# Attention block and large-kernel convolution on one core: padding columns left out, a mixed operand, and a new order of the first loads

## The chip, the cores and the metric

The kernel runs on one core of a Trainium2 chip. The metric is the device time of one execution in microseconds (us); the time before is the median of three runs. Beside it stands one profiled execution, from which all durations are read.

## What is computed

The input x has 384 channels of 192 x 192 pixels in float32. Two layers follow each other, each added to its own input:

```
x = x + L0(gn(x))        # gn: group normalization, 32 groups of 12 channels
x = x + L1(gn(x))

L0: qkv = w_qkv (1152 x 384) times the channels of every pixel, + bias
    2x2 max-pool  -> 96 x 96;  depthwise 3x3;  split in q, k, v
    8 heads of 48 channels: attn = normalized q times normalized k (48 x 48),
    four top-k softmaxes (24, 32, 36, 38 kept), summed with gains, times v
    exact GELU, 2x upsampling, w_proj (384 x 384), + bias
L1: sum of seven depthwise convolutions (13x13, and six dilated ones that fit
    inside 13x13), each with its own batch normalization
```

A head's 48 channels lie across the boundaries of the 128-channel tiles: heads 2 and 5 have channels in two tiles each.

## The kernel before, in words

**Stage 1, statistics (first 166 us).** The mean and variance of every channel are needed before anything can be normalized. The first 16 image rows are loaded as four large tiles xt (`load`, L160, on SP's DMA queue), which stay for the next stage. The rest comes as 66 blocks xs of 128 x 1536 (`load_block`, L201), on SP's queue for even numbers and ACT's for odd ones, ten buffers ahead. VectorE runs bn_stats over the four xt tiles (L230 to L234) and then over the 66 blocks in order (L235 to L241), with one bn_aggr for each channel tile (L243), and `group_stats` (L106) turns this into a scale and shift. Meanwhile GpSimd folds the seven convolution kernels into one (L217 to L225) and stores it as wfd (L226). The weights wqk and wv are loaded on SP's queue (L273, L274); these two lines lie outside a block of `manual_schedule`, so the framework's scheduler places them, and it placed them among the xs loads.

Inside a block of `tc.manual_schedule()` each engine executes its instructions in the order of the program text.

**Stage 2, attention (166 to 1951 us).** A list of steps (L629) goes twice over 24 blocks of the image: 12 steps a block for q and k, then six for v. A step is one `project` (L333, 12 records on TensorE) and its `pool` (L349). Depthwise taps (`taps`, L379, VectorE), `begin`, `end`, transposes (`turn`) and `add_gram` are put into later steps by `at(step, ...)`. In between, `normalize` prepares the next block on ACT, `add_up` forms 2x2 sums on GpSimd, and `strip` (L437) and `clear` (L288) lay out the convolution's tap matrices zd in DRAM: a load of wfd into the still free memory of v for every eighth block, one ACT copy, four DMA issues on GpSimd. The softmaxes (`attend`, L465) run inside the second pass and leave bd, the attention matrix of all heads as one block-diagonal matrix in three channel tiles.

**Stage 3, attention times v (1951 to 2060 us).** For 24 blocks of four rows (L702) TensorE multiplies bd with v. AV_BLOCKS (L47) lists which channel tiles of v each output tile needs: (0, 1), (0, 1, 2) and (1, 2), seven products of 384 columns. ACT applies GELU in place into v, VectorE takes statistics of the stored sums.

**Stage 4, projection (2060 to 2223 us).** 72 blocks (L1013): three products, ACT's copy with bias to pjs and its store to pd, VectorE's cell (L1037) and bn_stats (L1038). The generators in `running` are moved on by one `yield` at every block (`advance`, L991): `derive` (L790), which forms the second normalization's parameters for one channel tile and contains `group_stats` with `rsqrt`; `load_rows` for the convolution's first tiles; `residual` (L906), which adds the upsampled L0 output to the input rows, in parts of three rows on GpSimd here. Then come `patch`, `normalize1` and `arrange` for tile 0.

**Stage 5, convolution (2223 us to the end).** 48 tiles of eight channels (L1089). An image is cut into patches so that the 13x13 kernel is a product with a 128 x 128 matrix for each of five row offsets g: `convolve` (L945) runs five accumulating products of 24 x 12 = 288 columns. The input d is xp, [channel, 51 row groups, 12]; row group 0 and row group 50 lie outside the image and are zeros, set once by `patches` (L761, L762). Offset g reads row groups g, g+2, ..., so group 0 is the first of g = 0 and group 50 the last of g = 4. Around it the loop loads rows and taps ahead (SP), adds residuals (GpSimd), normalizes (ACT), transposes in and out (VectorE) and stores (GpSimd's queue).

Of the kernel before, what the change touches and what calls it, by code (L numbers as in the profile page):

```python
# [14 lines left out]
P = 128  # L15
# [31 lines left out]
AV_BLOCKS = [  # L47
    [
        j
        for j in range(NJ)  # L50
        if any(
            CH * h < P * (j + 1) and CH * (h + 1) > P * j and CH * h < P * (i + 1) and CH * (h + 1) > P * i
            for h in range(HEADS)
        )
    ]
    for i in range(NJ)
]
# [3 lines left out]
def tile_attn_then_large_kernel_conv(ctx: ExitStack, tc: tile.TileContext, a: dict, out: bass.AP):  # L61
# [24 lines left out]
    def rsqrt(pool, v, eps, name, least=None):  # L86

        shape = list(v.shape)
        ve = pool.tile(shape, F32, name=f"{name}_ve")
        if least is None:  # L90
            nc.vector.tensor_scalar(ve, v, eps, None, ALU.add)
        else:
            nc.vector.tensor_scalar(ve, v, least, None, ALU.max)
        sd = pool.tile(shape, F32, name=f"{name}_sd")
        nc.scalar.activation(sd, ve, AF.Sqrt)
        r = pool.tile(shape, F32, name=f"{name}_r")
        nc.vector.reciprocal(r, sd)

        t = pool.tile(shape, F32, name=f"{name}_t")
        nc.vector.tensor_mul(t, r, r)  # L100
        nc.vector.tensor_mul(t, t, ve)
        nc.vector.tensor_scalar(t, t, -0.5, 1.5, ALU.mult, ALU.add)
        nc.vector.tensor_mul(r, r, t)
        return r

    def group_stats(pool, psum, mv, name, js=range(NJ)):  # L106
# [25 lines left out]
        r = rsqrt(pool, var, 1e-5, name)  # L132
# [38 lines left out]
    with (  # L171
# [29 lines left out]
        def load_block(n):  # L201
            j, b = divmod(n, NX)
            xt = sx.tile([P, FB], F32, name=f"xs_{n}", tag="xs")
            eng = nc.sync if n % 2 == 0 else nc.scalar
            eng.dma_start(out=xt, in_=x[j * P : (j + 1) * P, FX + b * FB : FX + (b + 1) * FB])
            xss.append(xt)

        scale = rsqrt(s1, bn[:, :, 3, :], 1e-5, "bn")
# [8 lines left out]
        for j in range(NJ):  # L217
# [8 lines left out]
        nc.gpsimd.dma_start(  # L226
            out=wfd.rearrange("(j p) s -> p j s", p=P), in_=wf.rearrange("p j x y -> p j (x y)")
        )

        for n in range(4):  # L230
            xt = xts[n // 2, n % 2]
            for j in range(NJ):
                nc.vector.bn_stats(stats[:, j, 2 * n, :], xt[:, j, :512])
                nc.vector.bn_stats(stats[:, j, 2 * n + 1, :], xt[:, j, 512:])  # L234
        for n in range(NJ * NX):  # L235
            j, b = divmod(n, NX)
            xt = xss.pop(0)
            for q in range(FB // 512):
                nc.vector.bn_stats(stats[:, j, NS0 + b * (FB // 512) + q, :], xt[:, q * 512 : (q + 1) * 512])  # L239
            if n + 10 < NJ * NX:  # L240
                load_block(n + 10)  # L241
            if b == NX - 1:
                nc.vector.bn_aggr(mv0[:, j, :], stats[:, j].rearrange("p n s -> p (n s)"))  # L243
        nc.vector.tensor_copy(gn0, in_one(group_stats(s1, s_ps, mv0, "g0")))  # L244
# [7 lines left out]
    with ExitStack() as ctx_v:  # L252
# [20 lines left out]
        nc.sync.dma_start(out=wqk, in_=wqkv[:, :, : 2 * C])  # L273
        nc.sync.dma_start(out=wv, in_=wqkv[:, :, 2 * C :])  # L274
# [359 lines left out]
        with tc.manual_schedule():  # L634
            for sb in range(2):
                for j in range(NJ):
                    normalize(0, sb, j)
                    add_up(0, sb, j)
            for s, (B, u, m, sb) in enumerate(steps):
# [11 lines left out]
                if B < NB and u == 3:  # L651
                    strip(b)
                if B + 1 < 2 * NB:
# [31 lines left out]
        with (  # L685
# [13 lines left out]

            with tc.manual_schedule():  # L700
                sms = [load_sums(b) for b in range(2)]
                for b in range(NBB):  # L702
                    if b + 2 < NBB:
                        sms.append(load_sums(b + 2))
                    pss = []
                    for i in range(NJ):
                        ps = b1_ps.tile([P, NBK], F32, tag=f"av{i}", name="av")
                        js = AV_BLOCKS[i]
                        for j in js:
                            nc.tensor.matmul(  # L710
                                ps,
                                lhsT=bd[:, j, i * P : (i + 1) * P],
                                rhs=v[:, j, b * RB : (b + 1) * RB, :].rearrange("p r w -> p (r w)"),
# [3 lines left out]
                        pss.append(ps)  # L717
                    for i in range(NJ):
# [36 lines left out]
        def patches(pool, i):  # L755
# [5 lines left out]
            nc.gpsimd.memset(t[:, :, 0], 0.0)  # L761
            nc.gpsimd.memset(t[:, :, NQ - 1], 0.0)  # L762
# [27 lines left out]
        def derive(i, stats):  # L790
# [27 lines left out]
            for q, t in enumerate((mean, sd)):  # L818
                nc.gpsimd.tensor_copy(sv[:, q], t.unsqueeze(2).to_broadcast([P, nj, P]))
# [86 lines left out]
        def residual(k, n=ME + 1):  # L906

            for m0 in range(0, ME + 1, n):
# [3 lines left out]
                nc.gpsimd.tensor_add(rv, rv, uv.unsqueeze(2).to_broadcast([P, (m1 - m0) * WS, 2]))  # L912
# [32 lines left out]
        def convolve(k, c, co):  # L945
# [3 lines left out]
            for g in range(NGR):  # L949
                o = (NGR - 1 - g) * UQ * BC  # L950
                nc.tensor.matmul(  # L951
                    ps,
                    lhsT=wt[:, c, o : o + P],
                    rhs=d[:, c, g : g + 2 * NT - 1 : 2, :],
                    start=(g == 0),
# [42 lines left out]
        with (  # L998
# [4 lines left out]
            with tc.manual_schedule():  # L1003
# [9 lines left out]
                for n in range(NJ * NBB):  # L1013
# [38 lines left out]
                    if n == NBB + 13:  # L1052
                        running.append(residual(0, 3))
# [11 lines left out]
                    if n == 2 * NBB + 12:  # L1065
                        running.append(residual(1, 3))
                    if n == 3 * NBB - 4:
                        assert next(first, first) is first
# [93 lines left out]
```

## Time and profile before

| what | value |
|---|---|
| median of three runs (range) | 3169.14 us (3168.58 to 3170.71) |
| the profiled execution | 3174.78 us |
| its span, first to last instruction | 3172.9 us |
| mean granted TensorE clock | 0.997 |
| statistics end, first product | 159.1, 166.8 us |
| attention times v | 1951.0 to 2060.2 us |
| projection | 2060.2 to 2223.5 us |
| convolution's products begin | 2223.5 us |

The profile names instructions by line, engine and operation, with output and inputs by the program's names. PE is TensorE, PEld its weight load, DVE VectorE, POOL GpSimd, SP the engine that only issues DMAs. "The chain" is the sequence of work that ended last, followed back from the last instruction. An arrow at the end of a line (`<-`) names what ended the idle time before it. A float32 product appears as two TensorE records. The granted clock (PEclk) is 1.00 at full speed.

### The profile page before, as it was taken

What the parts mean: (1) busy time and instruction counts of PE and PEld (TensorE: products, weight loads), DVE (VectorE), ACT (ScalarE), POOL (GpSimd) and SP (SyncE); (2) the same over time, 40 slices, a digit from 0 to 9 for tenths busy, and PEclk for the clock granted to TensorE, in tenths of its full rate; (3) what the DMA queues carried; (4) which work ended last, traced back from release to release, by engine and by line L of the source; (5) the groups of instructions that cost most, each with busy time, mean ns of one, the idle gap of its engine ahead of it and who ended that gap; (6) DMA issues with size and microseconds to landing.
All of it is one profiled execution on the core that took longest, in us unless ns stands there. A gap on an engine that the chain in (4) does not pass through costs nothing.

```text
span 3172.9 us, 31552 instructions
## 1 busy us (share of the span) xinstructions
PE 2982.8 (94%) x10954; PEld 1971.5 (62%) x10954; DVE 2497.1 (79%) x3387; ACT 1227.9 (39%) x2288; POOL 878.5 (28%) x1044
## 2 busy tenths in 40 slices
PE   0099999999999999999999999999999999999998
PEld 0056666666666666665555555555777777777776
DVE  7968787878878787889998988366788777777775
ACT  0044444444444444444445443323333333333332
POOL 3033232332323223212222221011333343333331
PEclk9999999999999999999999999999999999999999
DMA  9924444343443434333333333376999999999994
GB/s 386 372 84 125 127 122 115 109 121 113 125 128 116 118 111 117 116 103 123 100 97 123 104 109 110 116 213 190 256 256 242 237 244 242 241 244 242 241 215 113
DMA packets 274960, 528.65 MB, mean 167 GB/s; under 512 B 22290, under 2 KB 189664, under 8 KB 274800
## 3 DMA queue, kind: packets, MB, share of 16 engines
q1 hardware_dynamic: 203664, 333.91, 39.1%
q0 software_dynamic: 45104, 152.26, 17.3%
q10 hardware_dynamic: 26032, 40.46, 3.5%
q8 instruction: 86, 1.41, 0.2%
q14 instruction: 74, 0.61, 0.1%
HBM read 365.18 MB, written 161.37 MB: 166 GB/s over the span
## 4 chain that ended last, share of the span: by engine, by line
PE 87%; DVE 8%; DMA 3%; issue 1%; POOL 0%; ACT 0%; SPq 0%; POOLq 0%; DVEq 0%; ACTq 0%
PE qkv L340 48%; PE conv L951 28%; PE pj L1022 4%; PE av L710 3%; DVE v L387 3%; DVE stats L239 2%; PE gram L428 2%; PE tr L416 2%; DVE mx L351 1%; DMA xs<-in_x 1%; DMA xt<-in_x 1%; DMA wqk<-in_wqkvT 1%; DMA pd<-pjs 0%; DMA up<-pd 0%; DMA wt<-zd 0%
## 5 line engine op out<-in xcount | busy, mean ns | idle before, releaser
L340 PE MATMUL qkv<-xt,wqk 128*128 128x384 f32 x3456 | 1133.1, 487 | 1.3 <-ACT xt L317 1.3
L951 PE MATMUL conv<-xp,wt 128*128 128x288 f32 x3840 | 933.1, 406 | 1.2 <-ACT co L959 1.2
L340 PEld LDWEIGHTS qkv<-xt,wqk 128*128 128x128 f32 x3456 | 650.5, 190 | 436.0 <-ACT xt L317 2.1
L951 PEld LDWEIGHTS conv<-xp,wt 128*128 128x128 f32 x3840 | 729.0, 190 | 202.8 <-ACT co L959 1.7
L387 DVE SCALAR_TENSOR_TENSOR acc<-pooled,wd,acc 128x384 f32<-128x384 f32 (+2 forms) x1152 | 720.8, 626 | 30.6
L351 DVE TENSOR_REDUCE mx<-qkv 128x192 f32<-128x768 f32 x432 | 412.7, 955 | 253.4 <-PE qkv L340 241.2
L935 DVE STREAM_TRANSPOSE xp<-xn 128x4608 f32<-128x4608 f32 (+1 forms) x107 | 441.7, 4128 | 190.7 <-PE conv L951 171.6
L358 ACT ACTIVATE pooled<-mx,bq 128x192 f32<-128x192 f32 x432 | 196.8, 456 | 963.9 <-DVE mx L351 963.9
L340 PE MATMUL qkv<-xt,wv 128*128 128x384 f32 x1728 | 563.4, 487 | 1.5 <-ACT xt L317 1.1
L340 PEld LDWEIGHTS qkv<-xt,wv 128*128 128x128 f32 x1728 | 325.7, 190 | 234.3 <-ACT xt L317 7.1
L959 ACT ACTIVATE co<-conv,cb 128x288 f32<-128x288 f32 x384 | 191.3, 499 | 605.5 <-PE conv L951 605.5
L387 DVE SCALAR_TENSOR_TENSOR v<-pooled,wd,v 128x384 f32<-128x384 f32 (+2 forms) x576 | 375.5, 652 | 15.2
L325 POOL TENSOR_TENSOR sum<-xt 128x192 f32<-128x192 f32 x144 | 94.7, 657 | 699.6 <-ACT xt L317 699.1
L317 ACT ACTIVATE xt<-xt,gn 128x768 f32<-128x768 f32 x288 | 284.8, 1013 | 2.9 <-DVE gn L244 2.9
L976 POOL DMA_DIRECT2D out<-o x191 | 105.8, 584 | 585.0 <-DVE o L967 532.2
L912 POOL TENSOR_TENSOR raw<-raw,up 128x2496 f32<-128x2496 f32 (+2 forms) x56 | 241.9, 4325 | 22.4 <-DMA up<-pd 22.4
L967 DVE STREAM_TRANSPOSE o<-co 128x2304 f32<-128x2304 f32 (+1 forms) x50 | 209.8, 4199 | 20.5 <-ACT co L959 20.5
L456 POOL DMA_DIRECT2D zd<-v x96 | 72.0, 757 | 510.9 <-ACT v L447 510.9
L112 PE MATMUL g_ps<-mv,gm 128*32 128x1 f32 x18 | 1.8, 186 | 159.3 <-DVE mv L243 158.6
L1022 PE MATMUL pj<-v,wp 128*128 128x384 f32 x432 | 148.8, 504 | 2.6 <-DVE cell L1037 2.1
L239 DVE BATCH_NORM_STATS2 stats<-xs 128x6 f32<-128x512 f32 x198 | 118.4, 678 | 6.2 <-DMA xs<-in_x 5.4
L1022 PEld LDWEIGHTS pj<-v,wp 128*128 128x128 f32 x432 | 83.8, 197 | 60.4 <-issue 5.1
(165 smaller groups left out, 1751.8 us busy)
## 6 DMA issues: line engine op xcount, KB each, us to landing
xt<-in_x SPq DMA_DIRECT2D x96, 1152.0 KB, 5.6
wt<-zd SPq DMA_DIRECT2D x47, 1536.0 KB, 13.1
raw<-in_x SPq DMA_DIRECT2D x182, 312.0 KB, 12.8
out<-o POOLq DMA_DIRECT2D x188, 288.0 KB, 6.3
zd<-v POOLq DMA_DIRECT2D x96, 416.0 KB, 5.0
up<-pd SPq DMA_DIRECT2D x184, 156.0 KB, 11.8
xs<-in_x SPq DMA_DIRECT2D x33, 768.0 KB, 14.7
xs<-in_x ACTq DMA_DIRECT2D x33, 768.0 KB, 12.3
```

The costliest lines, as they stand in the source:

```text
L239: nc.vector.bn_stats(stats[:, j, NS0 + b * (FB // 512) + q, :], xt[:, q * 512 : (q + 1) * 512])
L317: nc.scalar.activation(xt[:, j], xt[:, j], AF.Identity, bias=gn0[:, j, 1:2], scale=gn0[:, j, 0:1])
L340: nc.tensor.matmul(ps[:, r, : 2 * W], lhsT=wq[:, j, mm * P : (mm + 1) * P], rhs=xt[:, j, r * 2 * W : (r + 1) * 2 * W], start=(j == 0), sto ...
L351: nc.vector.tensor_reduce(mx, ps[:, :, : 2 * W].rearrange("p r (y w x) -> p r w y x", y=2, x=2), AX.XY, ALU.max,)
L358: nc.scalar.activation(pool_t[m][:, k : k + SR, 1 : 1 + WS], mx, AF.Identity, bias=bq[:, m : m + 1])
L387: nc.vector.scalar_tensor_tensor(acc[:, :nt], pool_t[m][:, k0 + dy : k0 + dy + nt, dx : dx + WS], wd[:, m, t : t + 1], acc[:, :nt], ALU.mu ...
L912: nc.gpsimd.tensor_add(rv, rv, uv.unsqueeze(2).to_broadcast([P, (m1 - m0) * WS, 2]))
L935: nc.vector.transpose(bass.AP(at.tensor, at.offset, [list(at.ap[0]), [NBQ, n], [1, NBQ], [NQ * NBQ, CC], [ME * NBQ, NE]],), bass.AP(row.te ...
L951: nc.tensor.matmul(ps, lhsT=wt[:, c, o : o + P], rhs=d[:, c, g : g + 2 * NT - 1 : 2, :], start=(g == 0), stop=(g == NGR - 1),)
L959: nc.scalar.activation(co[:, c], ps, AF.Identity, bias=cb[:, cc : cc + 1])
L967: nc.vector.transpose(bass.AP(at.tensor, at.offset, [list(at.ap[0]), [2 * W, n], [BC, NBQ], [W, 2], [1, BC]]), bass.AP(of.tensor, of.offse ...
L1022: nc.tensor.matmul(ps, lhsT=wp[:, j, i * P : (i + 1) * P], rhs=v[:, j, b * RB : (b + 1) * RB, :].rearrange("p r w -> p (r w)"), start=(j = ...
```

## The change

1. The convolution's products with g = 0 and g = 4 leave out the row block that lies outside the image (23 x 12 columns instead of 24 x 12); g = 1 goes first, so that the first product of the accumulation writes all columns. The zeros in xp are no longer set.
2. The two 32-channel ends of v that the middle output tile needs from tiles 0 and 2 are copied by GpSimd into one operand hx, at the partitions they have anyway (96 to 127 and 0 to 31), and the matching rows of bd into bdx. The middle tile then takes two products instead of three. The operands are made two row blocks ahead, in three buffers, and cleared once by VectorE. The products and GELUs go in the order 0, 2, 1.
3. The first six xs blocks go to ACT's DMA queue, of the others the even ones to SP's; VectorE takes the xt tiles between the first blocks. wfd is stored on SP's queue after the loads, wqk loaded behind it, wv at step 8. `strip` goes from step 3 of a block to step 8.
4. `rsqrt` works in place and yields once between the square root on ACT and the rest. `derive` broadcasts with VectorE instead of GpSimd. The residuals of the convolution's tiles 0 and 1 are added by VectorE; those of tile 1 are spread over blocks from 2*NBB+8.

```diff
+LO = P - P // CH * CH
+HI = (2 * P // CH + 1) * CH - 2 * P
+AV_BLOCKS = ((0, 1), (1, NJ), (1, 2))
...
-    def rsqrt(pool, v, eps, name, least=None):
+    def rsqrt(pool, v, eps, name):
...
-        nc.scalar.activation(sd, ve, AF.Sqrt)
         r = pool.tile(shape, F32, name=f"{name}_r")
-        nc.vector.reciprocal(r, sd)
+        nc.scalar.activation(r, ve, AF.Sqrt)
+        yield
+        nc.vector.reciprocal(r, r)
...
-        r = rsqrt(pool, var, 1e-5, name)
+        r = yield from rsqrt(pool, var, 1e-5, name)
...
-            eng = nc.sync if n % 2 == 0 else nc.scalar
+            eng = nc.scalar if n < 6 or n % 2 == 1 else nc.sync
...
-        nc.gpsimd.dma_start(
-            out=wfd.rearrange("(j p) s -> p j s", p=P), in_=wf.rearrange("p j x y -> p j (x y)")
-        )
-
-        for n in range(4):
+        def rows_stats(n):
             xt = xts[n // 2, n % 2]
...
         for n in range(NJ * NX):
+            if n in (0, 1, 3, 5):
+                rows_stats((n + 1) // 2)
...
+        nc.sync.dma_start(
+            out=wfd.rearrange("(j p) s -> p j s", p=P), in_=wf.rearrange("p j x y -> p j (x y)")
+        )
...
-        nc.sync.dma_start(out=wqk, in_=wqkv[:, :, : 2 * C])
-        nc.sync.dma_start(out=wv, in_=wqkv[:, :, 2 * C :])
...
         with tc.manual_schedule():
+            nc.sync.dma_start(out=wqk, in_=wqkv[:, :, : 2 * C])
...
-                if B < NB and u == 3:
+                if B < NB and u == 8:
                     strip(b)
+                if s == 8:
+                    nc.sync.dma_start(out=wv, in_=wqkv[:, :, 2 * C :])
...
+            hx = [b1.tile([P, NBK], F32, name=f"hx{n}") for n in range(3)]
+
+            def mix(b):
+
+                for t, q, j in ((P - LO, P, 0), (0, HI, 2)):
+                    nc.gpsimd.tensor_copy(
+                        hx[b % 3][t:q], v[t:q, j, b * RB : (b + 1) * RB, :].rearrange("p r w -> p (r w)")
+                    )
+
+            bdx = b1.tile([P, P], F32, name="bdx")
             with tc.manual_schedule():
+                for t in [bdx] + hx:
+                    nc.vector.memset(t, 0.0)
+                nc.scalar.copy(bdx[P - LO :], bd[P - LO :, 0, P : 2 * P])
+                nc.scalar.copy(bdx[:HI], bd[:HI, 2, P : 2 * P])
                 sms = [load_sums(b) for b in range(2)]
+                for b in range(2):
+                    mix(b)
                 for b in range(NBB):
                     if b + 2 < NBB:
+                        mix(b + 2)
...
-                    for i in range(NJ):
+                    for i in (0, 2, 1):
...
-                                lhsT=bd[:, j, i * P : (i + 1) * P],
-                                rhs=v[:, j, b * RB : (b + 1) * RB, :].rearrange("p r w -> p (r w)"),
+                                lhsT=bd[:, j, i * P : (i + 1) * P] if j < NJ else bdx,
+                                rhs=v[:, j, b * RB : (b + 1) * RB, :].rearrange("p r w -> p (r w)")
+                                if j < NJ
+                                else hx[b % 3],
...
-            nc.gpsimd.memset(t[:, :, 0], 0.0)
-            nc.gpsimd.memset(t[:, :, NQ - 1], 0.0)
...
-                nc.gpsimd.tensor_copy(sv[:, q], t.unsqueeze(2).to_broadcast([P, nj, P]))
+                nc.vector.tensor_copy(sv[:, q], t.unsqueeze(2).to_broadcast([P, nj, P]))
...
-        def residual(k, n=ME + 1):
+        def residual(k, eng=nc.gpsimd, n=ME + 1):
...
-            for g in range(NGR):
+            for g in (1, 0, 2, 3, 4):
+                t0, t1 = int(g == 0), NT - int(g == NGR - 1)
                 o = (NGR - 1 - g) * UQ * BC
                 nc.tensor.matmul(
-                    ps,
+                    ps[:, t0:t1],
                     lhsT=wt[:, c, o : o + P],
-                    rhs=d[:, c, g : g + 2 * NT - 1 : 2, :],
-                    start=(g == 0),
+                    rhs=d[:, c, g + 2 * t0 : g + 2 * t1 - 1 : 2, :],
+                    start=(g == 1),
...
-                        running.append(residual(0, 3))
+                        running.append(residual(0, nc.vector, 3))
...
-                    if n == 2 * NBB + 12:
-                        running.append(residual(1, 3))
+                    if n == 2 * NBB + 8:
+                        second = residual(1, nc.vector, 3)
+                    if n >= 2 * NBB + 8 and (n % 3 == 2 or n > 2 * NBB + 16):
+                        next(second, None)
```

## The prediction

> **What bounds the kernel now.** I read the page's busy times and chain first, then the chain in order of time, then windows of each stage, and last the timeline at the places where the change cuts in.
>
> ```profile
> PE 2982.8 (94%) x10954; PEld 1971.5 (62%) x10954; DVE 2497.1 (79%) x3387; ACT 1227.9 (39%) x2288; POOL 878.5 (28%) x1044
> ...
> PE qkv L340 48%; PE conv L951 28%; PE pj L1022 4%; PE av L710 3%; DVE v L387 3%; DVE stats L239 2%; PE gram L428 2%; PE tr L416 2%; DVE mx L351 1%; DMA xs<-in_x 1%; DMA xt<-in_x 1%; DMA wqk<-in_wqkvT 1%; DMA pd<-pjs 0%; DMA up<-pd 0%; DMA wt<-zd 0%
> ```
> TensorE carries the span except for the first 166 us. So a column taken out of a product pays directly, and so does every wait put in front of one. The chain in order of time (start, us, what):
> ```profile
> 50.17 18.29 DMA wqk<-in_wqkvT
> ...
> 117.78 39.12 DVE stats L239 x66
> ...
> 293.88 34.86 PE qkv L340 x108
> ...
> 1950.97 108.64 PE av L710 x336
> ...
> 2133.36 4.73 DVE dd L812
> ...
> 2261.81 39.00 PE conv L951 x160
> ```
> A float32 product counts as two records. From these lines, one record of 384 columns costs 34.86/108 = 0.3228 us, one of 288 columns 39.00/160 = 0.2438 us: 0.0790 us for 96 columns, 0.823 ns a column, almost nothing fixed. Windows (us, PE, PEld, DVE, ACT, POOL busy, granted clock, DMA share, GB/s):
> ```profile
> 15.00:20.00 5.00, 0.00 (x0) 0.00 (x0) 2.23 (x5) 0.00 (x0) 5.00 (x15) 1.00 1.02 371
> 140.00:150.00 10.00, 0.00 (x0) 0.00 (x0) 10.00 (x18) 0.00 (x0) 0.00 (x0) 1.00 1.00 411
> 150.00:160.00 10.00, 0.61 (x4) 0.53 (x4) 9.20 (x14) 0.00 (x0) 0.00 (x0) 1.00 0.04 17
> 2249.00:3141.00 892.00, 891.86 (x3695) 698.49 (x3696) 699.24 (x529) 310.79 (x508) 325.74 (x232) 1.00 0.98 237
> ```
> The first stage is DMA at its limit until 150 us, with VectorE's statistics ending behind it; the convolution is TensorE without a gap.
>
> **Columns outside the image (convolution).** 384 calls lose one of 24 row blocks (12 of 288 columns) in two of five products: 384 x 2 x 2 records = 1536, each 12 x 0.823 = 9.9 ns shorter: **15.2 us**. If time went strictly with columns it would be 15.6; if a record had a floor, less. The weight load (190 ns in its row) stays under the new 234 ns, so I see no floor. The stage must also be able to run faster, 0.32 us a tile of channels (19.4 us). DMA share 0.98 looks full, but the DMA queue's own waits say otherwise:
> ```profile
> SPq L895 <- PE conv L951: 178.4, 34, 9.0
> ```
> In 34 turns SP sat 178.4/34 = 5.2 us each, waiting for TensorE to free the tap buffer. DVE waits 147.8/34 = 4.3 us a turn for TensorE. Both hide the 0.32. The four memsets of xp (0.18 us each) go; POOL waits 17 us for a DMA just behind the second pair, so they are worth nothing.
>
> **One operand fewer in attention times v.** 24 row blocks lose one product of 384 columns: 48 records x 0.3233 (108.64/336) = 15.5 us. Added per block: two GpSimd copies of 32 partitions x 384. No row of before shows one; bounds are 0.45 us (128x256 copy, L819) and 0.77 us (2.0 ns an element from L912's two-input 5.02 us for 2496). I take 0.5, the nearest form, so 1.0 us a block beside TensorE's 12 x 0.323 = 3.9: hidden, if made two blocks ahead. It is not hidden in the first block. The operand tiles and bdx are cleared on VectorE, and VectorE is late there:
> ```profile
> 1950.97 9.30 PE L710 MATMUL av<-v,bd 128*128 128x384 f32 x28 [1.05 <-DVE mx L351]
> ...
> 1951.58 7.54 DVE L387 SCALAR_TENSOR_TENSOR v<-pooled,wd,v 128x384 f32<-128x384 f32 x11
> 1959.15 0.17 DVE L731 RECIPROCAL t<-gn 128x3 f32<-128x3 f32 x1
> ```
> TensorE starts this stage at 1951.0, while VectorE still has taps until 1959.1. Behind them come memset bdx (128 columns, about 0.25 by the 0.23 us copy L786) and hx0 (0.4; bounds 0.2 and 0.45, DVE copies of 64 and 256 elements): 1959.8. Then GpSimd's two copies: 1960.9. ACT's two copies into bdx (about 0.3 each, by 0.34 for 128x192) are beside that, with the Gelus queued behind them. TensorE has 10 records before it needs the mix: 1951.0 + 3.2 = 1954.2. It stands **6.8 us**. An idle of that length also costs clock. The windows show 0.50 granted for 3.3 us after an idle of 3.7 (2123.6 to 2127.3) and for 6.6 us after one of 2.9 (2135.3 to 2138.2). [...] by the worse row 3.3. I take 1.7, which the first row gives too. [...] Net: 15.5 - 6.8 - 1.7 = **7.0 us** (4 to 9; 15 if the clears could go ahead of the taps). The Gelus' new order moves nothing: three of 0.49 stay three.
>
> **Statistics in order of landing.** wqk (1.18 MB), wv (0.59) and wfd (0.94) go behind x; six blocks move to ACT's queue, so SP carries 4 large tiles and 30 blocks (28.3 MB) and ACT 36 blocks (28.3); before it was 32.4 with the weights against 26.0. The first 20 us move 5 x (111+395+323+371) = 6.0 MB, after that 415 GB/s. x (56.6) and small inputs (0.7) are then complete at 20 + 51.3/0.415 = 143.6 us, against 150 before, or 148.7 if wfd and wqk, queued on SP behind its last block, compete with ACT's last blocks. VectorE's own work is 198 x 0.594 (39.12/66) + 11.3 (x tiles) + 6.5 (aggregates) = 135.4; from its start at 8.2 it can't end before 143.6, plus some 6 of waiting for first data (now 15). Behind the last landing are about two blocks and an aggregate, 5.8 us. So the statistics end between 149.4 and 154.5, against 159.1. I take 151: **8 us** (4 to 10). wqk then lands at about 149 to 151, needed 7.7 us after the statistics (166.8 - 159.1): hidden by that. wv is needed at 1440.
>
> **The stage of the projection (2060 to 2223.5).** Its 432 records cost 139.5 us, the stage 163.4; the rest is stalls and half clock. The residual adds of the first two tiles and the sv copies go from GpSimd to VectorE; rsqrt gives way once more between ACT's square root and VectorE's part.
> ```profile
> 2133.06 5.47 POOL L912 TENSOR_TENSOR raw<-raw,up 128x576 f32<-128x576 f32 x5
> 2133.23 4.85 DVE L812 TENSOR_TENSOR dd<-of,chp 128x32 f32<-128x32 f32 x1
> 2138.22 0.60 PE L823 MATMUL pp<-dd,spread 128*128 128x32 f32 x2 [2.90 <-DVE dd L812]
> ```
> dd, 32 columns, lasts 4.85 us while GpSimd adds. [...] by the row the 2.9 us stall and 3.1 us of half clock behind it. I follow the row but credit **4**, as the taps' load (370 GB/s at 2136 to 2141) holds pjs stores then too. The other stall (3.7 idle, 1.6 of half clock, for L140's operand) has congested DMAs as its root, at 330 to 371 GB/s; with one more step TensorE can do another block first. I credit **2.5** (0 to 4). New on VectorE: per residual four adds of 576 and one of 192. No row at that size; 0.35 us at 192 and 0.18 at 21 give 1.0 ns an element, 0.74 for 576, 3.3 us in all. VectorE has 1.94 - 1.17 = 0.77 us free per block; with transposes on the other turns it runs full for some turns. Behind a late add stand the cell and statistics operations that free PSUM (three buffers); cost 0.5 (0 to 2). sv, 6 copies of 0.3 to 0.45 with dd behind them, fits the same gap. Net **6 us** (0 to 9). The idle at 2180 comes from the loads of tile 1, which stay.
>
> **Moved and hidden.** strip goes from step 3 to 8: one ACT copy (1.75 us), four GpSimd issues (0.76 each), one SP load in eight. In steps 6 to 11 ACT has some 2.3 us of work in 3.87; with strip 4.1, so it is 0.2 late once and recovers 1.5 a step, and TensorE needs the normalized tiles only later. Uncovered: 24 x 0.2 = 5 us. GpSimd is 1.8 us late behind add_up, then waits anyway (699 us for L317 in all). wfd and wqk are two issues of 0.4 us on SP, ahead of nothing due; GpSimd loses one of 0.84. The third derive ends one turn later, with over ten turns to spare.
>
> **Sum.** 8 + 7 + 6 + 15.2 = 36.2 us. Against the profiled run (3174.8 around a span of 3172.9) 3138.6; the median of the runs shown is 5.6 lower, so **3132.9**; own range 3124 to 3142.
>
> **Rivals.** (a) The stall at 1954 does not occur, as clears are placed ahead of the taps: 8.5 better, 3124.4. For: the mask copy (L772) slipped in at 1951.46. Against: clears and taps lie in blocks ordered by hand. (b) The start gives nothing, its end set by VectorE or a late wqk: 3140.9. For: VectorE has no gap from 83 to 157 us, and 135 us of work. (c) The convolution doesn't follow its columns, because its DMA has no more to give or a record has a floor: the change then does half of what it says, 3148.1. For: share 0.98. Against: SP's wait, and 286 GB/s in 2249 to 2288. (d) Slower: the mix becomes the pace of attention times v. It decides when a pair of copies exceeds 3.9 us; to use up the other 29 + 15.5 - 8.5 us and end above 3175.5, the pair must take about 5.7 us (24 x 1.8 = 43). For: GpSimd's spans are rough[...]. Against: 2.8 us a copy is four times the highest row[...].
>
> **Chances.** Forecast 0.62, (a) 0.13, (b) 0.12, (c) 0.08, (d) 0.05, of which 0.02 within 0.2% (6.3 us, about what a measurement of this kernel can tell from no change). Range 3120 to 3148 takes in (a), (b) and the better half of (c). Faster 0.95, same 0.02, slower 0.03.
>
> **What would show it.** Conv: 3840 records with 1536 of 276 columns, the stage 15 shorter and still without PE gaps; an SP wait gone and ACT or DVE waiting for DMA would mean (c). Attention: 288 av records, a PE idle of 6 to 7 us some 3 us into the stage, released by GpSimd or ACT, then half clock. Start: the first product at about 159, wqk not in the chain. Projection: dd under 1 us, stage near 157. Wrong if PE waits per block for hx, or if the start's DMA tail still runs to 150 with statistics behind it.

## The result and the profile after

The changed kernel takes **3152.12 us** (median of four runs, 3151.22 to 3152.71); the kernel before took 3169.93 beside it (3168.58 to 3170.97). The ratio is 0.9944 (95% interval 0.9927 to 0.9961): 17.8 us faster where 36.2 were forecast, and above the range's upper end of 3148. The profiled execution took 3152.71 us around a span of 3150.9, at a clock of 0.996.

The kernel before is itself not steady: measured again beside each of the four later groups of experiments, its median was 3173.14, 3173.43, 3174.51 and 3173.95, single runs from 3166 to 3177. So each experiment is compared with the runs of the kernel before that were made beside it. The traces are compared by stage:

| us from the span's start to the first product, then by stage | before | after | difference | forecast |
|---|---|---|---|---|
| start | 166.8 | 166.0 | -0.8 | -8 |
| q, k, v | 1784.2 | 1783.6 | -0.6 | 0 |
| attention times v | 109.2 | 103.1 | -6.1 | -7.0 |
| projection | 163.3 | 161.1 | -2.2 | -6 |
| convolution (start of the first to start of the last product) | 936.4 | 923.9 | -12.5 | -15.2 |
| tail | 13.0 | 13.2 | +0.2 | 0 |

The parts fell short everywhere, most of all the start, which gave nearly nothing. One row needs care: the projection's stage scatters. In the four profiles that hold it as it was before (before itself and three of the experiments below) it took 163.3, 162.6, 160.0 and 159.2 us, so 2.2 us between two profiles say little. The page's busy times, and the chain of after in order of time (start, us, what):

```profile
PE 2952.2 (94%) x10906; PEld 1962.4 (62%) x10906; DVE 2506.1 (80%) x3407; ACT 1229.4 (39%) x2290; POOL 896.7 (28%) x1071
```
```profile
5.55 12.32 DMA xs<-in_x
17.89 26.95 DMA xs<-in_x
44.86 28.59 DVE stats L230 x48
...
116.94 39.12 DVE stats L230 x66
...
1959.62 92.52 PE av L723 x278
...
2108.15 11.84 DMA pd<-pjs
...
2232.67 4.92 POOL raw L925
2237.61 2.15 ACT xn L933
2240.20 13.88 PE conv L966 x50
2254.36 38.36 PE conv L966 x160
```
TensorE is busy 30.6 us less, more than the span gained: it does less work, and waits more. The chain names the waits: an xs load of 27 us at the start, no wqk; an av group that begins 10 us after the stage did; a pjs store that took 11.8 us; and an addition to raw with ACT's normalization (xn), behind which TensorE goes on in the middle of the convolution's second tile.

**Start.** The timeline of SP's queue, then VectorE's (the bracket is the idle time before the line, and what ended it):
```profile
14.12 0.37 SPq L627 DMA_DIRECT2D wqk<-in_wqkvT  x1
17.89 30.17 SPq L196 DMA_DIRECT2D xs<-in_x  x6
```
```profile
44.86 28.58 DVE L230 BATCH_NORM_STATS2 stats<-xs 128x6 f32<-128x512 f32 x48 [7.24 <-DMA xs<-in_x]
156.09 2.16 DVE L234 BATCH_NORM_AGGREGATE mv<-stats 128x2 f32<-128x444 f32 x1
```
wqk goes out ahead of SP's first xs block, not behind the last. VectorE, done with the blocks of ACT's queue, waits 7.24 us for that block, and from 44.86 us on has no gap to 158.3, where the statistics end (159.1 before). The DMA was lighter at the end, as forecast (353 GB/s in 140 to 150 us, 411 before), but it no longer set the end.

**Attention times v.** The timeline at the stage's start:
```profile
1949.56 3.49 PE L723 MATMUL av<-v,bd 128*128 128x384 f32 x10 [1.05 <-DVE mx L343]
1950.17 7.54 DVE L379 SCALAR_TENSOR_TENSOR v<-pooled,wd,v 128x384 f32<-128x384 f32 x11
1957.99 1.19 DVE L707 MEMSET hx<- 128x384 f32 x3
1958.51 4.46 POOL L700 COPY hx<-v 32x384 f32<-32x384 f32 x8 [8.29 <-DVE hx L707]
1959.61 0.50 PEld L723 LDWEIGHTS av<-hx,bdx 128*128 128x128 f32 x2 [7.18 <-POOL hx L700]
1959.62 1.65 PE L723 MATMUL av<-hx,bdx 128*128 128x384 f32 x2 [6.56 <-DVE quarter L747]
1961.06 3.41 PE L723 MATMUL av<-v,bd 128*128 128x384 f32 x5
```
Ten records, then TensorE stands 6.56 us for hx, which waits for the clear, which waits for the taps: the order the forecast gave. (The bracket of the product names a VectorE line that ended just then; the weight load of the same product, one line up, was released by GpSimd's copy into hx.) Seven records then take 4.85 us (to 1964.47) where 7 x 0.323 = 2.3 is normal, so 2.6 go to half clock (0.50 granted from 1960 to 1964).

**Projection.** The stall stands ahead of g_pc, a small product inside `derive`; its operand g_sb comes from VectorE's reciprocal behind ACT's square root. TensorE's line of before, then of after:
```profile
2127.30 0.57 PE L140 MATMUL g_pc<-g_sb,gmt 32*128 32x2 f32 x2 [3.73 <-DVE g_sb L135]
```
```profile
2122.96 0.58 PE L130 MATMUL g_pc<-g_sb,gmt 32*128 32x2 f32 x2 [4.93 <-DVE g_sb L125]
```
VectorE's timeline round it, with one line of ACT's; GpSimd's before and after; and windows of after (us, busy PE, PEld, DVE, ACT, POOL, granted clock, DMA share, GB/s):
```profile
2116.44 0.14 DVE L83 TENSOR_SCALAR g_ve<-g_var 32x1 f32<-32x1 f32 x1
2120.07 0.58 ACT L1045 ACTIVATE pjs<-pj,bpj 128x384 f32<-128x384 f32 x1 [3.02 <-DMA pd<-pjs]
2120.68 0.61 DVE L1052 SCALAR_TENSOR_TENSOR cell<-smj,quarter,pj 128x384 f32<-128x384 f32 x1 [4.10 <-ACT pjs L1045]
2121.80 0.14 DVE L87 RECIPROCAL g_r<-g_r 32x1 f32<-32x1 f32 x1
2122.77 0.14 DVE L125 SCALAR_TENSOR_TENSOR g_sb<-g_mean,g_r 32x1 f32<-32x1 f32 x1
```
```profile
2130.38 0.29 POOL L819 COPY sv<-mean 128x128 f32<-128x128 f32 x1 [15.82 <-DVE mean L809]
2132.09 0.94 POOL L895 DMA_DIRECT2D wt<-zd  x1 [1.20 <-issue]
```
```profile
2108.20 0.94 POOL L908 DMA_DIRECT2D wt<-zd  x1
```
```profile
2116.00:2120.00 4.00, 2.03 (x7) 0.88 (x6) 0.55 (x3) 1.03 (x2) 0.00 (x0) 1.00 1.03 384
2122.00:2124.00 2.00, 1.04 (x3) 1.00 (x4) 0.77 (x6) 0.36 (x1) 0.00 (x0) 0.50 0.67 216
```
The dd stall is gone (0.17 us, 4.85 before). In its place TensorE waits 4.93 us for g_sb (3.73 before), with half clock behind it (0.50 in 2122 to 2124). ACT's square root was done at 2117.0, but the reciprocal stands behind a cell that waits for ACT's pjs, and that for the landing of an earlier store, while rows and taps fill the DMA (share 1.03 in 2116 to 2120). The taps' load, held behind the sv copies until 2132.09 before, now goes out at 2108.20.

**Convolution.** Groups by shape (count, busy time, mean ns, idle time before):
```profile
L966 PE MATMUL conv<-xp,wt 128*128 128x288 f32 x2304 | 686.1, 407 | 2.4 <-ACT co L974 2.4
L966 PE MATMUL conv<-xp,wt 128*128 128x276 f32 x1536 | 483.1, 396 | 0.0
```
1536 short records, and 160 records take 38.36 us instead of 39.00; over 3840 that is 15.4. About 2.8 are given back at one wait, of 2.35 us (1.22 before), behind which 50 records take 13.88 us where 12.19 is the undisturbed time (the clock is 0.50 in 2242 to 2244). TensorE's lines, before and after:
```profile
2249.14 12.39 PE L951 MATMUL conv<-xp,wt 128*128 128x288 f32 x50 [1.22 <-ACT co L959]
```
```profile
2240.20 13.88 PE L966 MATMUL conv<-xp,wt 128*128 128x288 f32 x50 [2.35 <-ACT co L974]
```
The wait comes 100 records into the stage, inside the second tile (a tile has 80). It is for ACT, which cannot empty TensorE's results because it stands, in its order, before the normalization of the third tile's rows, until GpSimd has added to them (a wait of 8.77 us, to 2237.61).

### The profile page after: what moved, and what is told of

Read it like the earlier page. It is cut to its first block, busy times and chain, and to the rows that moved or that the text cites. A ratio compares the mean times of both kernels' runs of the same rounds, so it can differ in the third digit from the quotient of the medians.

```text
span 3150.9 us, 31869 instructions
## 1 busy us (share of the span) xinstructions
PE 2952.2 (94%) x10906; PEld 1962.4 (62%) x10906; DVE 2506.1 (80%) x3407; ACT 1229.4 (39%) x2290; POOL 896.7 (28%) x1071
## 4 chain that ended last, share of the span: by engine, by line
PE 86%; DVE 9%; DMA 3%; issue 1%; ACT 0%; POOL 0%; ACTq 0%; DVEq 0%; POOLq 0%
PE qkv L332 49%; PE conv L966 28%; DVE stats L230 3%; DVE v L379 3%; PE pj L1037 3%; PE av L723 3%; PE gram L420 2%; PE tr L408 2%; DMA xs<-in_x 1%; DMA pd<-pjs 1%; DVE mx L343 1%; DMA up<-pd 0%; DVE cell L1052 0%; DVE mv L234 0%; ACT pjs L1045 0%
## 5 line engine op out<-in xcount | busy, mean ns | idle before, releaser
L966 PE MATMUL conv<-xp,wt 128*128 128x288 f32 (+1 forms) x3840 | 919.4, 403 | 2.4 <-ACT co L974 2.4
L379 DVE SCALAR_TENSOR_TENSOR acc<-pooled,wd,acc 128x384 f32<-128x384 f32 (+2 forms) x1152 | 732.3, 636 | 30.6
L379 DVE SCALAR_TENSOR_TENSOR v<-pooled,wd,v 128x384 f32<-128x384 f32 (+2 forms) x576 | 375.6, 652 | 15.2
L925 POOL TENSOR_TENSOR raw<-raw,up 128x2496 f32<-128x2496 f32 x46 | 231.1, 5025 | 23.1 <-DMA raw<-in_x 18.2
L318 POOL TENSOR_TENSOR sum<-sum,xt 128x192 f32<-128x192 f32 x144 | 113.2, 786 | 11.3
## 6 DMA issues: line engine op xcount, KB each, us to landing
wt<-zd SPq DMA_DIRECT2D x47, 1536.0 KB, 13.2
```

The source lines that it names most:

```text
L379: nc.vector.scalar_tensor_tensor(acc[:, :nt], pool_t[m][:, k0 + dy : k0 + dy + nt, dx : dx + WS], wd[:, m, t : t + 1], acc[:, :nt], ALU.mu ...
L925: eng.tensor_add(rv, rv, uv.unsqueeze(2).to_broadcast([P, (m1 - m0) * WS, 2]))
L966: nc.tensor.matmul(ps[:, t0:t1], lhsT=wt[:, c, o : o + P], rhs=d[:, c, g + 2 * t0 : g + 2 * t1 - 1 : 2, :], start=(g == 1), stop=(g == NGR ...
```

## The experiments

**The four parts alone**, each as the diff of the change shows it (only its main lines are shown here), on the kernel before. Before beside them: 3173.14 us (31 runs).

```diff
-                    rhs=d[:, c, g : g + 2 * NT - 1 : 2, :],
+                    rhs=d[:, c, g + 2 * t0 : g + 2 * t1 - 1 : 2, :],
```


> The kernel before with the shorter products alone. In the changed kernel a record of 276 columns takes 0.2338 us against 0.2438 (groups of 160 records: 38.36 against 39.00 us), so 1536 records are worth 15.4 us. Theory: part of that is given back at the start of the convolution, because TensorE now comes sooner to the place where ACT waits for the first residual, stands longer there and loses clock: 12.6 us faster, the idle near the 100th record above 2 us. Rival: that stall belongs to another part of the change; then 15 us faster, the idle as before (1.3 us).

3157.49 us, ratio 0.9952 (0.9937 to 0.9967): -15.7 us, stage 921.4 (-15.0). The wait inside the second tile was 1.51 us, and the 50 records behind it took 12.19: no clock lost. So the rival came true and not the theory, and the columns are worth what was forecast.

```diff
-AV_BLOCKS = [
...
+AV_BLOCKS = ((0, 1), (1, NJ), (1, 2))
```


> The kernel before with the mixed operand alone. Theory: 15.5 us of products saved, about 6 us of standing for the clears and copies plus half clock behind it: 6 us faster, an idle of 6 us some 3 us into the stage. Rival (the stall is an artefact of the other parts): 12 to 15 us faster.

3168.54 us, ratio 0.9987 (0.9978 to 0.9996); the stage took 103.4 (-5.8), as in the full change.

```diff
-        r = rsqrt(pool, var, 1e-5, name)
+        r = yield from rsqrt(pool, var, 1e-5, name)
...
-                nc.gpsimd.tensor_copy(sv[:, q], t.unsqueeze(2).to_broadcast([P, nj, P]))
+                nc.vector.tensor_copy(sv[:, q], t.unsqueeze(2).to_broadcast([P, nj, P]))
...
+                        running.append(residual(0, nc.vector, 3))
```


> The kernel before with only the projection stage's part: one more yield in rsqrt, sv and two residuals on VectorE. Theory: taking sv off GpSimd frees GpSimd's queue, so the load of the first taps starts some 20 us sooner and meets the row loads; pjs stores land late and TensorE stands about 5 us: 2 us faster (0 to 4), the tap load issued within 2 us of the last row load. Rival (the forecast): 6 us faster, no stall above 2 us near that place.

3172.99 us, ratio 1.0000 (0.9992 to 1.0009), stage 164.5 (163.3 before): nothing. The taps went out at 2116.28, dd took 0.17 us, and TensorE waited 2.53, 3.16, 2.07 and 3.04 us. The part trades one stall for others.

```diff
-            eng = nc.sync if n % 2 == 0 else nc.scalar
+            eng = nc.scalar if n < 6 or n % 2 == 1 else nc.sync
...
+            nc.sync.dma_start(out=wqk, in_=wqkv[:, :, : 2 * C])
```


> The kernel before with only the start's part: blocks on ACT's queue, statistics in order of landing, wfd, wqk, wv and strip moved. Theory: wqk is placed on SP's queue ahead of SP's first block, VectorE stands some 7 us for that block and then has no gap to the end: 0 to 2 us faster, first product at about 166. Rival (the forecast): 8 us faster, first product at 159.

3170.80 us, ratio 0.9996 (0.9988 to 1.0005), first product at 166.1 (-0.7). wqk went out at 13.79 us, ahead of SP's blocks, and VectorE waited 7.28 us for the first of them. The projection, not touched here, took 159.2: that stage scatters by some 4 us by itself. dd lasted 3.03 us here, and TensorE waited 0.24 us for it; in before it lasted 4.85, with a wait of 2.90.

The four gains by the medians are 15.7 + 4.6 + 0.1 + 2.3 = 22.7; the whole change gave 17.8 and, measured again later, 21.1. Within that scatter the parts add up; what is lacking is lacking in each part.

**One repair for each shortfall**, on the changed kernel. Before beside them: 3173.43 us.

```diff
+        nc.sync.dma_start(out=wqk, in_=wqkv[:, :, : 2 * C])
         nc.vector.tensor_copy(gn0, in_one(group_stats(s1, s_ps, mv0, "g0")))
...
-            nc.sync.dma_start(out=wqk, in_=wqkv[:, :, : 2 * C])
```
(inside the block of the statistics, behind the store of wfd, with a memory pool of its own)

> The changed kernel with wqk in a memory of its own and its load written into the statistics' block, so that it really stands behind all xs loads on SP's queue. Theory: VectorE's stall of 7.2 us for SP's first block goes, the statistics end near 152 instead of 158.3: 5 to 7 us faster than the changed kernel (about 3146). Rival: VectorE or the DMAs set the end whatever stands first; less than 2 us.

3147.31 us, ratio 0.9920 (0.9905 to 0.9935); first product at 161.4, -4.6. SP's queue, and VectorE's lines, the first of which answers to the one with 7.24:
```profile
18.11 115.36 SPq L199 DMA_DIRECT2D xs<-in_x  x30
136.92 0.38 SPq L238 DMA_DIRECT2D wfd<-wf  x1
137.35 0.48 SPq L241 DMA_DIRECT2D wqk<-in_wqkvT  x1
```
```profile
39.48 28.84 DVE L233 BATCH_NORM_STATS2 stats<-xs 128x6 f32<-128x512 f32 x48 [1.09 <-DMA xs<-in_x]
111.73 39.70 DVE L233 BATCH_NORM_STATS2 stats<-xs 128x6 f32<-128x512 f32 x66
151.47 2.16 DVE L237 BATCH_NORM_AGGREGATE mv<-stats 128x2 f32<-128x444 f32 x1
```
With wqk really behind, SP's first block is issued no earlier (18.11 us, 17.89 in the changed kernel) but is there 5.4 us earlier, the wait for it shrinks to 1.09 us, and the statistics end at 153.6. This is the order that the forecast had costed at 151. Its chain runs through xs loads again, from 109.6 to 140.7, but hardly anything is waited for: VectorE's last 66 records take 39.70 us, 39.20 in the changed kernel. Its own work and the waits at the start set the end even in this order.

```diff
-            hx = [b1.tile([P, NBK], F32, name=f"hx{n}") for n in range(3)]
...
-                for t in [bdx] + hx:
-                    nc.vector.memset(t, 0.0)
...
+                if B == 2 * NB - 4 and u == 0:
+                    for t in hx:
+                        nc.vector.memset(t, 0.0)
+                if B == 2 * NB - 3 and u == 0:
...
+                    for q in range(2):
+                        mix(q)
```


> The changed kernel with hx and bdx cleared, bdx copied and the first two mixes made during the last blocks of the v pass. Theory: TensorE's idle of 5.4 to 6.6 us in attention times v and the 2 us of half clock behind it go: 7 to 9 us faster than the changed kernel. Rival: something else is late there (the memory of the closed pools, ACT): under 3 us.

3143.02 us, ratio 0.9906 (0.9891 to 0.9921); the stage takes 93.8, -9.3. At the place of the stall:
```profile
1949.73 3.49 PE L727 MATMUL av<-v,bd 128*128 128x384 f32 x10 [1.05 <-DVE mx L343]
1953.06 0.81 PE L727 MATMUL av<-hx,bdx 128*128 128x384 f32 x2
```
No wait between them: stall and clock together were worth 9.3 (6.6 + 2.6 by the trace; the forecast had 8.5).

```diff
-            load_taps(1)
             patches(l2, 1)
             all_of(load_rows(2))
+            load_taps(1)
```


> The changed kernel with the rows of tile 2 loaded ahead of the taps of tile 1 at the start of the convolution. Theory: the first residual starts about 5 us sooner, the 2.4 us stall and the half clock behind it go: 3 to 4 us faster than the changed kernel. Rival: the taps are then late and TensorE stands at tile 1: no gain or a loss of some us.

3150.48 us, ratio 0.9930 (0.9915 to 0.9945). The convolution takes 919.6, -4.3, and in its chain the records of the first two tiles (150) are one piece, with the next following at once:
```profile
2215.26 35.77 PE conv L966 x150
2251.31 38.36 PE conv L966 x160
```
So the wait came from the rows of tile 2 (the third, counted from 0), queued on SP behind the taps of tile 1. The time gained less than the stage; in its profile the projection took 162.6.

```diff
-                nc.vector.tensor_copy(sv[:, q], t.unsqueeze(2).to_broadcast([P, nj, P]))
+                nc.gpsimd.tensor_copy(sv[:, q], t.unsqueeze(2).to_broadcast([P, nj, P]))
```


> The changed kernel with only the sv copies back on GpSimd. They hold GpSimd's queue until VectorE has the mean, so the tap load is issued some 20 us later, as before; the residuals stay on VectorE[...]. Theory: pjs stores land in under 6 us, the 4.9 us stand of TensorE shrinks to 2 or less and its half clock goes: 3 to 6 us faster than the changed kernel. Rival (the stall comes from the extra yield or from the row loads alone): within 1 us.

A miss: 3151.06 us, ratio 0.9932 (0.9915 to 0.9949), stage 160.6. The taps still went out at 2108.31, since rsqrt's extra step puts the sv copies behind them in GpSimd's order. So it told nothing about the loads' collision; GpSimd's timeline shows why:
```profile
2108.31 0.94 POOL L908 DMA_DIRECT2D wt<-zd  x1
2127.43 0.28 POOL L832 COPY sv<-mean 128x128 f32<-128x128 f32 x1 [18.18 <-DVE mean L822]
```

**The projection, and all repairs.** Before beside them: 3174.51 us.

> The changed kernel once more, unaltered, as the baseline of this call and a second profile of it. Every theory expects 0.993 to 0.995 of the time before. Theory (each stall is fixed by the order of instructions): first product 166, attention times v 103, convolution 924 us as in the first profile, to within 1 us; the projection's stage, where DMAs of three queues race, anywhere from 159 to 165. Rival (the stalls themselves are accidents of one execution): one of the other stages is off by over 3 us too.

No edit. 3153.44 us, ratio 0.9937 (0.9923 to 0.9951). Stages 166.5, 103.1, 163.2, 922.1: the projection 2.1 above the first profile, the others near it (the convolution 1.8 below, its wait of 2.20 us having cost no clock: 12.19 us for the 50 records behind it). The stall took another form: 3.00 us for a cell, then 1.64 for g_sb.

```diff
+                    if n == 8:
+                        load_taps(0)
...
-                    if n == NBB + 9:
-                        load_taps(0, nc.gpsimd)
```


> The changed kernel, with the load of the first taps (1.5 MB) issued on SP's queue at block 8 of the projection instead of on GpSimd's at block 33, behind the row loads. Theory (the 4.9 us stall ahead of g_pc and its half clock come from taps and rows landing together with the pjs stores): the taps land by 2085, the DMA near 2108 to 2122 carries the rows alone, the g_pc stall falls under 2 us, no half clock there, the stage takes 155 to 158 us instead of 160 to 161, the time is 3 to 5 us under that of the changed kernel. Rival 1 (the rows alone, or rsqrt's extra step, make the stall): it stays at 4 to 5 us, no gain. Rival 2: the sums queued on SP behind the taps come late, cell waits for DMA near block 12, and the gain is spent there.

3149.21 us, ratio 0.9925 (0.9913 to 0.9938): -4.2 against after_again beside it, stage 159.1. Half of the theory held: the wait ahead of g_pc fell to 2.91 us, but not under 2, and half clock stayed (0.50 in 2122 to 2126). The rows alone keep the DMA at a share of 1.04 from 2108 to 2116.

```diff
-        r = yield from rsqrt(pool, var, 1e-5, name)
+        r = in_one(rsqrt(pool, var, 1e-5, name))
...
-                nc.vector.tensor_copy(sv[:, q], t.unsqueeze(2).to_broadcast([P, nj, P]))
+                nc.gpsimd.tensor_copy(sv[:, q], t.unsqueeze(2).to_broadcast([P, nj, P]))
```


> The changed kernel with two parts of the projection's edit undone: the sv copies on GpSimd again and rsqrt without the extra step, so that the sv copies stand ahead of the taps' load in GpSimd's order as before. Theory (the sv copies held the taps' load back, until VectorE had the mean): the taps are issued at 2118 or later, the pjs stores near 2110 land sooner, the stall ahead of g_pc is again about 3 to 4 us for the mean's operand, dd stays under 1 us since the residuals are VectorE's, the stage takes 157 to 160 us. Rival (the extra step made the stall longer by itself, not the load): the taps are issued at 2108 as after and the stall is under 3 us. Rival (the load's place does not matter): issued later, and stall and stage as after.

3152.74 us, ratio 0.9931 (0.9918 to 0.9944), stage 160.7, a miss at its upper edge. The taps went out at 2122.44 and the wait ahead of g_pc fell to 2.57 (3 to 4 expected), but a wait of 2.76 us at 2170 with half clock behind it (six records in 4.21 us) followed, and one of 2.60 at the convolution's second tile; they took the gain back.

> The changed kernel with all four repairs: wqk behind the last x block on SP, the operands of attention times v cleared and first mixed inside the second pass, the rows of tile 2 ahead of the taps of tile 1, the first taps at block 8. Theory (the four shortfalls are separate and add up): 4.7 + 9.2 + 4.3 + 3 = some 21 us under the changed kernel, 3129 to 3134, first product 161.4, attention times v 93.8, projection 156 to 158, convolution 919.6. Rival (a stall taken away moves to the next stage): under 15 us, with one of the stages longer than in its own run.

Edit: s1, a1, c1 and p2 together. 3133.93 us, ratio 0.9874 (0.9860 to 0.9887), -19.5 against after_again. First product 161.3, attention times v 93.7, convolution 920.4: three repairs add up (4.7, 9.4 and 3.5 us; alone 4.6, 9.3 and 4.3). The projection took 159.9, and a wait of 3.42 us ahead of g_pc was back.

**The extra step alone, and with the taps.** Before beside them: 3173.95 us. Left open was how much of the g_pc stall was the extra step's.

```diff
-        r = yield from rsqrt(pool, var, 1e-5, name)
+        r = in_one(rsqrt(pool, var, 1e-5, name))
```


> The changed kernel with only rsqrt's extra step undone: the square root on ACT and VectorE's reciprocal stand in one block again; sv stays on VectorE, the taps' load on GpSimd at block 33. Theory (the step set the reciprocal behind the next block's cell, which waits for ACT's pjs, and that for the landing of an earlier pjs store): the reciprocal follows the root at once, the wait ahead of g_pc falls from 4.9 to under 3.5 us; as PSUM is full by then, TensorE is still held by the cell, so the gain is 1 to 2 us, and half clock stays. Rival 1 (the loads alone make the stall): still 4 to 5 us. Rival 2 (the step alone made it): no idle over 1 us and no half clock between 2112 and 2130, 3 to 5 us gained in the stage.

3151.11 us, ratio 0.9928 (0.9914 to 0.9941), stage 158.9. VectorE's timeline:
```profile
2116.51 0.61 DVE L1052 SCALAR_TENSOR_TENSOR cell<-smj,quarter,pj 128x384 f32<-128x384 f32 x1 [4.51 <-ACT pjs L1045]
2118.43 0.15 DVE L87 RECIPROCAL g_r<-g_r 32x1 f32<-32x1 f32 x1 [0.49 <-ACT g_r L85]
2120.56 0.62 DVE L1052 SCALAR_TENSOR_TENSOR cell<-smj,quarter,pj 128x384 f32<-128x384 f32 x1 [1.01 <-ACT pjs L1045]
```
The reciprocal follows the root and goes ahead of the late cell; the wait ahead of g_pc is 3.30, the stage 2.2 shorter than in the first profile of after, half clock stays (0.50 in 2120 to 2124). As the theory had it, and neither rival. One profile would not carry this, but six hold the changed kernel's order at this place (after, after_again, s1_wqk_behind, p1_sv_on_gpsimd, a1_clears_early, c1_rows_before_taps): there TensorE's waits sum to 4.45 to 6.10 us, and the stage takes 159.9 to 163.2.

> The changed kernel with the extra step undone and the first taps loaded at block 8 on SP. Theory (step and collision both count, each hides the other): wait ahead of g_pc under 1.5 us, no half clock before 2130, the stage takes 155 to 157 us, some 4 to 5 us under the changed kernel. Rival (the row loads alone fill the DMA, and PSUM runs full behind late pjs stores whatever else is done): a stall of 2 to 3 us and half clock stay, the stage at 158 to 160 us.

Edit: p2 and p4. 3147.20 us, ratio 0.9916 (0.9902 to 0.9929), stage 157.3. The gains add, but a wait of 2.50 us and a short half clock (0.50 in 2120 to 2122) remain: between the theory and its rival. The rows' own load is still there: ACT stands 4.34 us for a pjs store at 2111 to 2116 (in the chain that store takes 8.60 us, from 2107.14), with the taps issued long before (at 2070.2 in p2_taps_at_8, by the same edit).

> All four repairs, and the extra step undone as well. Theory: as all_moved with 2 us or more less in the projection's stage, 3129 to 3132 us. Rival: no different from all_moved (3133.9), since the projection's stage scatters by itself.

Edit: all_moved and p4. **3127.71 us**, ratio 0.9858 (0.9845 to 0.9872), the fastest here and 46 us under the kernel before; the projection took 153.9. TensorE's timeline there:
```profile
2102.37 0.38 PE L130 MATMUL g_pc<-g_sb,gmt 32*128 32x2 f32 x2 [0.76 <-DVE g_sb L125]
```
The stall is down to 0.76 us without half clock (1.00 in 2100 to 2104). In p5_both the same two edits left 2.50; the runs do not settle whether the earlier repairs changed the phase of the loads, or this is the stage's scatter.

## Why the prediction was wrong, step by step

**Start (8 forecast, 0.8 came): the step that failed, twice over.** "wfd and wqk, queued on SP behind its last block": the text of the program puts wqk at the head of the next hand-ordered block. That fixes its order inside that block, and not against the blocks before it. SP's first xs block was issued only at 17.89 us, 12 us behind the xt loads, and the scheduler put a later load into the gap: wqk here and in s0_start_alone, the small bpj (14.31 us) in s1_wqk_behind. The xs load could not go yet: the queue's waits put 11.7 us ahead of it down to the landing of an xt load. That the scheduler filled the gap for this reason is argued, not shown. I knew that the scheduler had placed wqk among the blocks before, and took it that the new place in the text ended this. And "plus some 6 of waiting for first data" was mis-sized: VectorE's idles after the first data are 3.02 + 1.63 + 1.96 + 0.56 + 7.24 = 14.4 us, with 8.3 before the first data 23 in all, as before. VectorE's work of 135.4 us and 23 of waiting make 158.3. Rival (b) named this, "its end set by VectorE", at 0.12. s1_wqk_behind gives 4.6 of the 8 back; there too 8.7 us of idles after the first data stood where 6 were taken, and VectorE, not the last landing, set the end.

**Attention times v (7.0; 6.1 came): right.** Product count, place, length and cause of the stall were as worked out (6.8 forecast, 6.56 measured); the copies took 0.50 us, the value taken. The clock term was 1.7, and 2.6 came; it is not fixed, for in s1_wqk_behind, c1_rows_before_taps and p2_taps_at_8 the same wait of 6.56 us cost 1.1 us less behind it (stage 102.0). a1_clears_early shows that the whole 9.3 was avoidable: rival (a)'s size was right, though it did not happen.

**Projection (6; 2.2 by the two profiles, nothing by p0_projection_alone): the right part removed, a new wait in its place.** dd fell to 0.17 us and the residual adds took 0.74, as taken. But "with one more step TensorE can do another block first" (credited 2.5) had the wrong sign. What another step lets in is also VectorE's cell of that block, ahead of the reciprocal; the cell waits for ACT (4.10 us), and ACT for a store (3.02 us). p4_no_step: without the step the wait is 3.30 us, with it 4.45 to 6.10 (all waits at this place), and the stage 158.9 us, with it 159.9 to 163.2. And the sv copies were costed by their own time alone. On GpSimd they held the queue, waiting 15.8 us for VectorE, and so held the taps' load (1.5 MB) clear of the row loads, to 2132.09. Moved to VectorE, they released it into them, at 2108.20. With the taps out of the way (p2_taps_at_8) the time is 4.2 us shorter, and 3.9 when the same edit is put on p4_no_step (p5_both). That holding them was better than releasing them is not shown: p3_no_yield and p4_no_step (measured in different groups) differ in nothing but the sv copies, and with the taps held to 2122.44 the wait is 2.57 instead of 3.30 us, but the stage 160.7 instead of 158.9. I had counted every queue that a moved instruction joins, and not the queue that it leaves. Also, the credit for dd rested on one profile of a race: in four profiles with GpSimd adding beside it, dd lasted 3.03 to 4.85 us, and TensorE's wait for it was 2.90, 2.85, 1.64 and 0.24 us.

**Convolution (15.2; 12.5 came): the mechanism and size right, the claim of full cover wrong.** c0_columns_alone gives 15.0 to 15.7. I had looked at SP's and VectorE's slack in the steady state. The first turn had none: TensorE waited 1.22 us, through ACT, for the rows of the third tile already before. Those loads go out from 0.7 us into the stage, before and after, while TensorE reaches the place 0.4 us sooner (100 records in 24.01 us instead of 24.41). With the short records alone the wait was 1.51 us. In the changed kernel GpSimd's addition also began 18.83 us into the stage instead of 18.11, the wait was 2.35 us, and it lost clock (13.88 us for the 50 records behind it). Why the rows came later is open; a0_operand_alone, with the long records, waited 1.93 us. c1_rows_before_taps removes the wait.

**strip, wv and the memsets, costed at nothing:** q, k, v moved by 0.6, so yes.

**The sum.** The forecast missed by 19.2 us. Against the profiled execution of before it gave 3138.6, and the profiled execution of after took 3152.7: 14.1 of the 19.2, of which the start makes 7.2, the projection 3.8, the convolution 2.7, the attention 0.9 and the tail 0.2, less 0.6 that came in q, k, v. The other 5 are the step from that profile to the median: I took off 5.6 us because before's three runs lay that much lower. The later medians of before, 3173.1 to 3174.5, lie only about 1 us under that profile, so by them the correction was some 4 us too large. The measured time lies nearest to rival (c)'s 3148.1, but (c) did not happen: the columns gave their 15 us.

## What to carry to other kernels

An instruction taken off an engine's queue releases what was queued behind it (here the taps' 1.5 MB, at 2108.20 instead of 2132.09 us): ask what that next instruction is and what it will collide with, above all if it is a large load. A place in the program's text is not a place in a queue (wqk went out at 14.12 us, ahead of SP's blocks): read in the trace when the load is issued, or put it inside the ordered block that it must follow. When a stage gets shorter, the loads for its first tiles do not (here they went out from 0.7 us on, as before, and TensorE came 0.4 us sooner): the slack of the first turn counts, not only that of the steady state. And a gain of 2 us in a stage that scatters by 4 (159.2 to 163.3 us here) is read from several profiles or from many runs, not from two traces.

## What was not expected of the hardware

Half clock after short idles is not a matter of their length alone. Waits of 1.87 us (p4_no_step, six records of 384 columns then in 3.90 us) and 2.15 us (the same run, 50 records in 13.88) were followed by it; waits of 2.17 (p5_both, 12.19), 2.20 (after_again, 12.19) and 2.52 us (p5_both, six records in 2.20) were not. What else decides it, no run here tests. A forecast of such a stall should carry both values, which by these runs lie about 1.7 us apart (3.90 and 2.20 us for six records, 13.88 and 12.19 us for 50).
